# Two graph layers, attention in bursts: both quads of a batch weighed and scored together, with sums over key blocks kept in place

## The chip, the cores and the metric

The kernel runs on one core of a Trainium2 chip. The core has a matrix engine (TensorE, PE in the profile, with its weight loads as PEld), three engines for elementwise work (VectorE or DVE, ScalarE or ACT, GpSimd or POOL), and queues that start transfers between the chip's main memory (HBM) and its working memory (SBUF). Matmuls write to a third memory, PSUM, which has eight banks of 512 float32 columns; VectorE and ScalarE read it. The metric is the device time of one execution in microseconds, lower is better.

## The reference

Two layers over 64 batches of 256 nodes with 512 features, each with a residual: a graph attention layer with one head, and a masked attention with eight heads of 64. All is float32.

```python
h = relu(layernorm(x));   x = x + gat(h)        # layer 0
h = relu(layernorm(x));   x = x + mha(h)        # layer 1

def gat(X):                                      # W: 512 x 256, a: 2 x 256
    h = X @ W
    e = leaky_relu(h @ a[0] + (h @ a[1]).T, 0.2)
    alpha = softmax(e masked where adj == 0)
    return concat([alpha @ h, h], -1)

def mha(h):                                      # 8 heads of 64
    q, k, v = heads(h @ Wq.T + bq), heads(h @ Wk.T + bk), heads(h @ Wv.T + bv)
    attn = softmax(where(adj == 0, -inf, q @ k.T / 8))
    return merge(attn @ v) @ Wo.T + bo
```

One adjacency matrix of 256 x 256 serves all batches.

## The kernel before

**Tiling and names.** The 64 batches are taken in `NG` = 32 groups of `GB` = 2. The 256 nodes of a batch are `NT` = 2 blocks of 128 partitions, the features `HP` = 4 blocks of 128. Eight heads make two "quads" of `QH` = 4 heads. `bounded` is the program that runs; `any_inputs` is a second program for inputs out of bounds, which doesn't run here.

**Products.** The projections to q, k and v (`project`, tiles `pq`, `pk`, `pv`) and the output projection (`outputs`, tile `py`) use seven products of half-sized blocks in place of eight. `operand_sums` makes four sums of blocks of the left operand (tile `sums` for q, k, v, on GpSimd; tile `o_sums` for the output, on VectorE), `weight_sums` makes those of the weights once, and `seven` says which block meets which. A product adds into a PSUM bank that is kept over several products (`held_bank`) or into one of the five banks of the tag `turn`, which `mm` hands out. Totals, weighed values, scores and the layer-0 products come from `turn` too. A float32 matmul shows in the trace as two passes.

**Attention of layer 1.** `scores(g, b, quad)` makes, for four heads of a batch, the transposed scores (keys on partitions): tile `sc`, matmuls of 64 rows (two heads side by side in the array), 512 columns for both key blocks. ScalarE takes the exponential into `p`, VectorE multiplies two heads at a time by the mask `maskT`, GpSimd adds the two key blocks into the tile `ps`. `weigh(g, b, quad, p, ps)` is called a step later: a matmul with ones (128 x 32) sums `ps` over the keys into `total`, VectorE takes the reciprocal `r`, sixteen matmuls with 128 x 32 blocks of v make the weighed values `pr`, and VectorE multiplies them by `r` into `oT`. After the second quad, `operand_sums` makes `o_sums` from the two `oT` tiles, and the output products of that batch can start.

**Layer 0.** `first_norm(g)` normalises and transposes x (by way of VectorE's block transposes and HBM, tiles `xn`, `xt`, `passed`, `moved`, `hT`). `first_layer(g)` makes `ph` = h @ W, then from a transposition `pn` the weights `e` (ScalarE, VectorE for leaky relu, ScalarE for the exponential, VectorE for the mask), then `po`, the weighed sum, and the second layernorm with its transposition.

**Order.** TensorE's order is the order in which the program calls `matmul` and `transpose`: each is tied to the one before. On the other engines a call by way of `not_sooner` stays behind the call before it; other calls are placed by the planner, by when it expects their inputs. The pieces are interleaved by strings, one for each step; a group has four steps (batch and quad):

```python
steps = ("Snuuuuonuouuo", "Sssnunosunosnouso", "Sususuososuos", "Ssusuonusonuouunous")
```

At the beginning of a step the quad of the step before is weighed. Then `S` is `scores` of this step, `u` a piece of the next group's projections (one product of seven), `o` a piece of the output products of the last batch weighed, `s` a piece of `first_layer` of the group after next, `n` a piece of a later group's first norm. So weighing and scores stand together four times in a group: totals, values and scores of one quad each.

**Buffers.** `p`, `ps`, `r`, `oT0` and `oT1` have one buffer each. `turn` has five PSUM banks.

Of the kernel before, what the change touches and what calls it, by code (L numbers as in the profile page):

```python
# [14 lines left out]
P = 128  # L15
# [42 lines left out]
def bounded(  # L58
# [102 lines left out]
    bad = const.tile([P, 2, NT], F32, name="bad")  # L161
    a_b = att.tile([P, 2, F1], F32, tag="ps", name="a_b", bufs=1)
    nc.sync.dma_start(
# [84 lines left out]
    gpsimd.memset(rexp, -0.5)  # L248
    ones = const.tile([P, P], F32, name="ones")
    gpsimd.memset(ones, 1.0)  # L250

    def weight_sums(name):
# [6 lines left out]
    def last_bias():  # L259


        wide = att.tile([P, 2, 2, P], F32, tag="kept", name="bv_wide")
        for q in range(NQ):
            for half in range(2):
                gpsimd.tensor_scalar(
                    wide[:, half, q, :], ones, bv_col[:, half, q : q + 1], None, op0=ALU.mult
                )
        yield
        pb = mm("pb")
        for q in range(NQ):  # L270
            for half in range(2):
                matmul(
                    pb, wide[:, half, q, :], w_sb["o"][:, half, 2 * q : 2 * q + 2, :],
                    start=(q == 0 and half == 0), stop=(q == NQ - 1 and half == 1),
                )
        yield
        not_sooner(vector, "tensor_add", b_out, pb, b_out)
        yield


    def judge():
# [41 lines left out]

        room = att.tile([P, D], F32, tag="ps", name="squares", bufs=1)

# [26 lines left out]
        total = mm("total")[:, :10]  # L352
        matmul(total, ones, part, start=True, stop=True)
        norm = const.tile([P, 10], F32, name="norm")
# [40 lines left out]
    def stats(mv, src, t, name):  # L395
        st = small.tile([P, 6], F32, tag="st", name=f"st{name}_{t}")
        if vector.last:
            not_sooner(vector, "bn_stats", st, src[t])
        else:
            vector.bn_stats(st, src[t])  # L400
        vector.bn_aggr(mv[:, t, :], st)

    def norm_T(src, mv, name, by_pe):
# [7 lines left out]
        def factors(b):  # L411
            tiles = slice(b * NT, (b + 1) * NT)
            ve = small.tile([P, NT], F32, tag="ve", name=f"ve{name}_{b}")
            vector.tensor_scalar(ve, mv[:, tiles, 1], EPS, None, op0=ALU.add)
            less = small.tile([P, NT], F32, tag="less", name=f"less{name}_{b}")
            vector.tensor_scalar(less, mv[:, tiles, 0], -1.0, None, op0=ALU.mult)
            rstd = small.tile([P, NT], F32, tag="rstd", name=f"rstd{name}_{b}")
            gpsimd.tensor_tensor(rstd, ve, rexp, op=ALU.pow)
            gpsimd.tensor_tensor(less, less, rstd, op=ALU.mult)
            factor[b] = less, rstd  # L420
# [51 lines left out]
    def operand_sums(engine, quads, sums):  # L472
        a11, a12, a21, a22 = quads
        not_sooner(engine, "tensor_add", sums[:, 0], a21, a22)
        engine.tensor_sub(sums[:, 1], sums[:, 0], a11)
        not_sooner(engine, "tensor_sub", sums[:, 2], a11, a21)
        engine.tensor_sub(sums[:, 3], a12, sums[:, 1])

    def seven(quads, sums):

        a11, a12, _, a22 = quads
        s1, s2, s3, s4 = (sums[:, i] for i in range(4))
        return {
            1: (a11, W11), 2: (a12, W21), 3: (s4, W22), 4: (a22, T4),
            5: (s1, T1), 6: (s2, T2), 7: (s3, T3),
        }
# [5 lines left out]
    def first_norm(g):  # L495

        xt = {}
        mv = small.tile([P, GT, 2], F32, tag="mv", name=f"mv0_{g}")
        factors, norm, turn, fetch, put = norm_T(xt, mv, f"0_{g}", g == 0)
# [34 lines left out]
    def first_layer(g):  # L534
# [30 lines left out]
        yield  # L565
        mv = small.tile([P, GT, 2], F32, tag="mv", name=f"mv1_{g}")
        factors, norm, turn, fetch, put = norm_T(xt, mv, f"1_{g}", g == 0)
        for r in range(GT):
            b, t = divmod(r, NT)
            po = mm(f"po_{g}_{r}")[:, : F1 + 1]  # L570
            for kb in range(NT):
# [3 lines left out]
                )  # L575
            ri = small.tile([P, 1], F32, tag="ri", name=f"ri_{g}_{r}")
            not_sooner(vector, "reciprocal", ri, po[:, F1:])
# [14 lines left out]
        hT = big.tile([P, HP, TOK], F32, tag="hT1", name=f"hT1_{g}")  # L592
        sums = big.tile([P, 4, 2, N], F32, tag="sums", name=f"sums_{g}", bufs=1)
        quads = [
# [111 lines left out]

    def scores(g, b, quad):


        (q, q_tag), (k, k_tag) = (qkv[name, g, b] for name in "qk")  # L710
        name = f"{g}_{b}_{quad}"
        p = att.tile([P, QH, NT, N], F32, tag="p", name=f"p_{name}", bufs=1)
        ps = att.tile([P, QH, N], F32, tag="ps", name=f"ps_{name}", bufs=1)
        for i in range(QH // 2):
            hp = quad * QH // 2 + i
            sc = [mm(f"sc_{name}_{2 * i + j}").rearrange("p (k n) -> p k n", k=NT) for j in range(2)]
            for kb in range(NT):
                for j in range(2):
                    rows = slice(j * DH, (j + 1) * DH)
                    matmul(  # L720
                        sc[j][:, kb, :], k[rows, hp, kb * P : (kb + 1) * P], q[rows, hp, :],
                        start=True, stop=True,
                    )
            pair = p[:, 2 * i : 2 * i + 2]
            for j in range(2):
                not_sooner(scalar, "activation", pair[:, j], sc[j], AF.Exp, scale=scale)
            vector.tensor_mul(pair, pair, maskT[:, None, :, :].to_broadcast([P, 2, NT, N]))
            not_sooner(
                gpsimd, "tensor_add", ps[:, 2 * i : 2 * i + 2, :], pair[:, :, 0, :], pair[:, :, 1, :]
            )  # L730
        if quad == NQ - 1:
            places.extend((q_tag, k_tag))
        return p, ps

    oTs = {}

    def weigh(g, b, quad, p, ps):


        v, v_tag = qkv["v", g, b]  # L740
        name = f"{g}_{b}_{quad}"
        total = mm(f"total_{name}")[:, :N]
        for j in range(QH):
            matmul(
                total[j * S : (j + 1) * S, :], ones[:, :S], ps[:, j, :], start=True, stop=True
            )
        r = att.tile([P, N], F32, tag="r", name=f"r_{name}", bufs=1)
        vector.reciprocal(r, total)
        pr = mm(f"pr_{name}").rearrange("p (h n) -> p h n", h=2)
        for half in range(2):  # L750
            for kb in range(NT):
                for j in range(QH):
                    c0 = (quad * QH + j) * DH + half * S
                    matmul(
                        pr[j * S : (j + 1) * S, half, :], v[:, kb, c0 : c0 + S], p[:, j, kb, :],
                        start=(kb == 0), stop=(kb == NT - 1),
                    )
        oT = big.tile([P, 2, N], F32, tag=f"oT{quad}", name=f"oT_{name}", bufs=1)
        vector.tensor_mul(oT, pr, r[:, None, :].to_broadcast([P, 2, N]))
        oTs[quad] = oT  # L760
        if quad == NQ - 1:
            places.append(v_tag)
            quads = [oTs[c][:, :, r * P : (r + 1) * P] for r in range(2) for c in range(2)]
            sums = big.tile([P, 4, 2, P], F32, tag="o_sums", name=f"o_sums_{g}_{b}", bufs=1)
            operand_sums(vector, quads, sums)
            operands["o", g, b] = seven(quads, sums)

# [96 lines left out]

    steps = ("Snuuuuonuouuo", "Sssnunosunosnouso", "Sususuososuos", "Ssusuonusonuouunous")
    waiting, late = None, iter(())
    for g in range(NG):
        products = project(g + 1) if g + 1 < NG else iter(())
        pieces = first_layer(g + 2) if g + 2 < NG else iter(())
        for step, parts in enumerate(steps):  # L870
            b, quad = divmod(step, NQ)
            if g == step == 0:

                parts = "Snn" + parts[2:].replace("uon", "unon", 1)
            if waiting is not None:
                weigh(*waiting)
                if waiting[2] == NQ - 1:
                    late = outputs(*waiting[:2])
            for part in parts:
                if part == "u":  # L880
# [3 lines left out]
                elif part == "s":  # L884
                    next(pieces, None)
                elif part == "n":
                    next(norms, None)
                else:
                    waiting = (g, b, quad, *scores(g, b, quad))
            if step == 0 and g + 1 < NG:  # L890
                residual(g + 1)
            if step % 2 == 0 and g + 3 < NG:
                load(g + 3, b)
        run(products)
# [374 lines left out]
```

## Time and profile before

| | |
|---|---|
| time, median of three runs | 2532.96 us (2532.34 to 2534.09) |
| span of the profiled execution | 2530.6 us |
| TensorE busy | 2500.6 us, 99% |
| VectorE busy | 1772.5 us, 70% |
| ScalarE busy | 1008.3 us, 40% |
| GpSimd busy | 952.0 us, 38% |
| DMA, mean over the span | 81 GB/s |
| instructions | 41538, of these 16158 matmul passes |

The profile is that of one execution. A row of its groups says: line, engine, operation, output<-inputs by tile name, shapes, count, then busy us and mean ns of one, then the idle time of the engine just before these instructions and what ended most of it. A line of the timeline has the start in us, the us that a run of equal instructions took, engine, line, operation, tiles, shapes and count. Line 35 is the helper through which VectorE, ScalarE and GpSimd are called, line 137 the one for matmuls, so groups are told apart by their tiles. The end of a matmul is modelled, and ends overlap the starts that follow: on TensorE, compare starts.

### The profile page before, as it was taken

Reading aid. Unit: us, or ns where it says so; the run is one execution under the profiler, and the core shown is the slowest. Engines: PE = TensorE matmul, PEld = TensorE weight load, DVE = VectorE, ACT = ScalarE, POOL = GpSimd, SP = SyncE. Lnnn points to the kernel's source line nnn. Section 1 sums busy time; section 2 is a strip of 40 time slices with the busy share of each in tenths; the row PEclk is TensorE's granted clock in tenths of the full one; section 3 lists DMA queues with packets and bytes.
Section 4 is the critical chain, followed back from the end, with each engine's and each line's share of the span. In section 5 each row is a group of like instructions: output and inputs, shape, how many; then the busy total and the mean of one; then the engine's idle time right before and its main releaser. Section 6 shows DMA issues by size and latency. Waiting matters only on the chain.

```text
span 2530.6 us, 41538 instructions
## 1 busy us (share of the span) xinstructions
PE 2500.6 (99%) x16158; PEld 2024.7 (80%) x16158; DVE 1772.5 (70%) x2971; ACT 1008.3 (40%) x2019; POOL 952.0 (38%) x913
## 2 busy tenths in 40 slices
PE   8899999999999999999999999999999999999998
PEld 7687888888788888888887888888888878888875
DVE  6577766776767777667767677776677676777655
ACT  5444334343343343343433433433434334334321
POOL 3433334333344333343333443333433334433332
PEclk9999999999999999999999999999999999999999
DMA  6222122331232321223312323212233123232100
GB/s 187 67 84 83 60 84 84 92 100 59 67 101 76 101 84 60 83 84 92 101 59 67 101 76 100 86 60 82 84 92 100 59 68 100 76 101 86 37 29 35
DMA packets 129352, 205.39 MB, mean 81 GB/s; under 512 B 13952, under 2 KB 78208, under 8 KB 129152
## 3 DMA queue, kind: packets, MB, share of 16 engines
q1 hardware_dynamic: 129152, 202.69, 25.5%
q8 instruction: 129, 2.11, 0.3%
q14 instruction: 71, 0.58, 0.1%
HBM read 104.08 MB, written 98.57 MB: 80 GB/s over the span
## 4 chain that ended last, share of the span: by engine, by line
PE 97%; DVE 1%; DMA 1%; POOL 0%; issue 0%; ACT 0%; SPq 0%; DVEq 0%; ACTq 0%; POOLq 0%
PE pq L137 15%; PE pk L137 15%; PE pv L137 15%; PE py L137 15%; PE sc L137 10%; PE ph L137 9%; PE pr L137 9%; PE po L137 4%; PE total L137 3%; PE pn L140 1%; DMA w_sb<-in_L_gnn_W_dram 0%; DVE p L35 0%; POOL ps L35 0%; PE gram_q L137 0%; PE gram_k L137 0%
## 5 line engine op out<-in xcount | busy, mean ns | idle before, releaser
L35 POOL TENSOR_TENSOR ps<-p 128x512 f32<-128x512 f32 x256 | 416.6, 1642 | 698.9 <-DVE p L35 698.9
L35 DVE TENSOR_TENSOR x<-py,x 128x256 f32<-128x256 f32 x448 | 186.5, 416 | 313.8 <-PE py L137 307.2
L35 ACT ACTIVATE p<-sc 128x512 f32<-128x512 f32 x512 | 264.3, 603 | 273.7 <-PE sc L137 273.7
L35 DVE TENSOR_TENSOR p<-p,maskT 128x1024 f32<-128x1024 f32 x256 | 333.7, 1334 | 49.5 <-ACT p L35 49.5
L35 ACT ACTIVATE xn<-x,less,rstd 128x512 f32<-128x512 f32 x256 | 194.9, 813 | 316.5 <-POOL less L35 316.5
L137 PE MATMUL sc<-q,k 64*128 64x256 f32 x2048 | 266.8, 390 | 0.0
L137 PE MATMUL py<-wo_sb,o_sums 128*128 128x256 f32 x1024 | 262.7, 380 | 2.6 <-DVE x L35 2.6
L35 DVE RECIPROCAL r<-total 128x256 f32<-128x256 f32 x128 | 224.6, 1755 | 44.6 <-PE total L137 44.6
L137 PEld LDWEIGHTS sc<-q,k 64*128 64x128 f32 x2048 | 195.9, 186 | 72.1 <-issue 52.6
L35 POOL TENSOR_TENSOR rstd<-ve,rexp 128x2 f32<-128x2 f32 x128 | 91.6, 716 | 428.9 <-DVE less L35 428.9
L137 PE MATMUL pr<-p,v 128*32 128x256 f32 x4096 | 245.5, 379 | 0.0
L137 PE MATMUL pv<-wv_sb,sums 128*128 128x256 f32 x1024 | 241.7, 379 | 2.7 <-ACT kept_v L35 2.7
L137 PE MATMUL ph<-w_sb,hT 128*128 128x258 f32 x1024 | 242.7, 384 | 0.4 <-ACT hT L35 0.3
L137 PE MATMUL pq<-sums,wq_sb 128*128 128x256 f32 x1024 | 238.2, 381 | 4.1 <-POOL sums L35 4.1
L137 PE MATMUL pk<-sums,wk_sb 128*128 128x256 f32 x1024 | 239.9, 382 | 0.0
L137 PEld LDWEIGHTS ph<-w_sb,hT 128*128 128x128 f32 x1024 | 191.8, 190 | 38.3 <-ACT p L35 9.6
L137 PEld LDWEIGHTS pk<-sums,wk_sb 128*128 128x128 f32 x1024 | 191.8, 190 | 35.8 <-issue 10.7
L137 PEld LDWEIGHTS pq<-sums,wq_sb 128*128 128x128 f32 x1024 | 195.3, 191 | 31.2 <-POOL sums L35 4.5
L137 PEld LDWEIGHTS pv<-wv_sb,sums 128*128 128x128 f32 x1024 | 194.5, 190 | 29.5 <-ACT kept_v L35 3.1
L137 PEld LDWEIGHTS py<-wo_sb,o_sums 128*128 128x128 f32 x1024 | 191.9, 190 | 29.1 <-DVE x L35 3.4
L137 PEld LDWEIGHTS pr<-p,v 128*32 128x32 f32 x4096 | 134.6, 110 | 86.7
L137 PE MATMUL py<-wo_sb,oT 128*128 128x256 f32 x768 | 197.1, 380 | 2.8 <-DVE x L35 2.8
(120 smaller groups left out, 3710.0 us busy)
## 6 DMA issues: line engine op xcount, KB each, us to landing
passed<-xt SPq DMA_DIRECT2D x124, 512.0 KB, 2.7
moved<-passed SPq DMA_DIRECT2D x496, 128.0 KB, 3.6
x<-in_x_dram SPq DMA_DIRECT2D x64, 512.0 KB, 4.9
out_dram<-x SPq DMA_DIRECT2D x64, 512.0 KB, 3.8
wq_sb<-in_L_gnn_Wq_dram SPq DMA_DIRECT2D x2, 512.0 KB, 9.4
wk_sb<-in_L_gnn_Wk_dram SPq DMA_DIRECT2D x2, 512.0 KB, 10.9
wv_sb<-in_L_gnn_Wv_dram SPq DMA_DIRECT2D x2, 512.0 KB, 7.5
wo_sb<-in_L_gnn_Wo_dram SPq DMA_DIRECT2D x8, 128.0 KB, 3.8
```

The lines of the kernel that those rows point to most:

```text
L35: instruction = getattr(self.engine, operation)(*args, **kwargs)
L137: in_order(nc.tensor.matmul(*args, **kwargs))
L140: in_order(nc.tensor.transpose(*args))
```

## The change

Two things are changed, and some tiles are moved or cut so that they fit.

First, `scores` and `weigh` take a whole batch. A group has two steps in place of four, with the same pieces in the same order but two `S` fewer. At the beginning of a step, TensorE does total, pr, total, pr (both quads of the batch before), and then eight heads of scores. The purpose is that the kinds of matmul that use the array in tiles (128 x 32 and 64 x 128) stand together half as often.

Second, with exponentials p0 and p1 of the two key blocks and values v0 and v1, p0 v0 + p1 v1 = (p0 + p1) v0 + p1 (v1 - v0). GpSimd's sum p0 + p1 is written over p0, so that the tile `ps` goes and `p` can hold eight heads. In return `value_differences` subtracts the first block of v from the second, in place, on GpSimd, once for each batch, in the middle of a group's first step. `total` reads its sums from `p`.

Third, for space: a21 - ... of the operand sums is written over a block that is not read again, so `sums` and `o_sums` have three blocks in place of four; the ones for `total` are 32 columns, and a square of ones lives for a while in the place of `o_sums`; setup tiles (`a_b`, `squares`) live in the places of `oT0` and `oT1`; small tiles are put together or have fewer buffers.

```diff
-    a_b = att.tile([P, 2, F1], F32, tag="ps", name="a_b", bufs=1)
+    a_b = big.tile([P, 2, F1], F32, tag="oT0", name="a_b", bufs=1)
...
-    ones = const.tile([P, P], F32, name="ones")
+    ones = const.tile([P, S], F32, name="ones")
     gpsimd.memset(ones, 1.0)
+    square_ones = big.tile([P, P], F32, tag="o_sums", name="square_ones", bufs=1)
+    gpsimd.memset(square_ones, 1.0)
...
-        st = small.tile([P, 6], F32, tag="st", name=f"st{name}_{t}")
+        st = small.tile([P, 6], F32, tag="st", name=f"st{name}_{t}", bufs=4)
...
-        not_sooner(engine, "tensor_sub", sums[:, 2], a11, a21)
-        engine.tensor_sub(sums[:, 3], a12, sums[:, 1])
+        not_sooner(engine, "tensor_sub", a21, a11, a21)
+        engine.tensor_sub(sums[:, 2], a12, sums[:, 1])
...
+    def value_differences(g):
+        for b in range(GB):
+            v = qkv["v", g, b][0]
+            not_sooner(gpsimd, "tensor_sub", v[:, 1, :], v[:, 1, :], v[:, 0, :])
+
-    def scores(g, b, quad):
+    def scores(g, b):
...
-        p = att.tile([P, QH, NT, N], F32, tag="p", name=f"p_{name}", bufs=1)
-        ps = att.tile([P, QH, N], F32, tag="ps", name=f"ps_{name}", bufs=1)
-        for i in range(QH // 2):
+        p = att.tile([P, NQ * QH, NT, N], F32, tag="p", name=f"p_{name}", bufs=1)
+        for i in range(HP):
...
-                gpsimd, "tensor_add", ps[:, 2 * i : 2 * i + 2, :], pair[:, :, 0, :], pair[:, :, 1, :]
+                gpsimd, "tensor_add", pair[:, :, 0, :], pair[:, :, 0, :], pair[:, :, 1, :]
...
-    def weigh(g, b, quad, p, ps):
+    def weigh(g, b, p):
...
+        for quad in range(NQ):
...
-                total[j * S : (j + 1) * S, :], ones[:, :S], ps[:, j, :], start=True, stop=True
+                    total[j * S : (j + 1) * S, :], ones, p[:, quad * QH + j, 0, :],
+                    start=True, stop=True,
...
-    steps = ("Snuuuuonuouuo", "Sssnunosunosnouso", "Sususuososuos", "Ssusuonusonuouunous")
+    steps = ("Snuuuuonuouuossnunosunosnouso", "Sususuososuossusuonusonuouunous")
...
-        for step, parts in enumerate(steps):
-            b, quad = divmod(step, NQ)
+        for b, parts in enumerate(steps):
...
             if waiting is not None:
                 weigh(*waiting)
-                if waiting[2] == NQ - 1:
-                    late = outputs(*waiting[:2])
+                late = outputs(*waiting[:2])
...
-            if step == 0 and g + 1 < NG:
-                residual(g + 1)
-            if step % 2 == 0 and g + 3 < NG:
-                load(g + 3, b)
+                if i == len(parts) // 2:
+                    if b == 0:
+                        if g + 1 < NG:
+                            residual(g + 1)
+                        value_differences(g)
+                    if g + 3 < NG:
+                        load(g + 3, b)
```

## The prediction

> **What bounds the kernel now.** I read the page first: busy shares, then the chain that ended last, then the costliest groups.
>
> ```profile
> PE 2500.6 (99%) x16158; PEld 2024.7 (80%) x16158; DVE 1772.5 (70%) x2971; ACT 1008.3 (40%) x2019; POOL 952.0 (38%) x913
> ...
> PE 97%; DVE 1%; DMA 1%; POOL 0%; issue 0%; ACT 0%; SPq 0%; DVEq 0%; ACTq 0%; POOLq 0%
> ...
> L35 DVE TENSOR_TENSOR p<-p,maskT 128x1024 f32<-128x1024 f32 x256 | 333.7, 1334 | 49.5 <-ACT p L35 49.5
> ...
> L35 DVE RECIPROCAL r<-total 128x256 f32<-128x256 f32 x128 | 224.6, 1755 | 44.6 <-PE total L137 44.6
> ...
> L35 POOL TENSOR_TENSOR x<-x,b_out 128x512 f32<-128x512 f32 x128 | 158.7, 1268 | 0.0
> ```
>
> The chain is TensorE from end to end. So only two things move the time: passes, or extra time between passes, on TensorE; and whatever makes TensorE wait. The change keeps the number of matmuls. So I looked at how passes follow each other, in the timeline of TensorE alone around one round of attention (total, pr, sc):
>
> ```profile
> 1035.44 1.89 PE L137 MATMUL pq<-hT,wq_sb 128*128 128x256 f32 x8
> 1037.17 1.89 PE L137 MATMUL pq<-sums,wq_sb 128*128 128x256 f32 x8
> 1038.89 1.03 PE L137 MATMUL py<-wo_sb,o_sums 128*128 128x256 f32 x4
> 1039.85 0.64 PE L137 MATMUL total<-ps,ones 128*32 128x256 f32 x8
> 1040.31 1.91 PE L137 MATMUL pr<-p,v 128*32 128x256 f32 x32
> 1042.14 2.00 PE L137 MATMUL sc<-q,k 64*128 64x256 f32 x16
> 1044.07 3.75 PE L137 MATMUL ph<-w_sb,hT 128*128 128x258 f32 x16
> 1047.66 0.59 PE L137 MATMUL pk<-hT,wk_sb 128*128 128x256 f32 x2
> ```
>
> Starts tell, not durations (their ends overlap). Eight full passes take 1.72 to 1.73 us, 0.2155 each. Four of py should take 0.86; the next start comes after 0.96, so going from 128*128 to 128*32 costs 0.10. Two rows of four concurrent passes of total take 0.46 (0.43 + 0.03). Eight such rows of pr take 1.83 (1.72 + 0.10), eight pairs of sc 1.93 (1.72 + 0.20), and the sixteen ph passes (258 columns) 3.59 against 3.48 (+0.11). The costs gather where the tile shape changes: 0.10 + 0.10 + 0.20 + 0.11, about 0.5 us a round. There are two rounds to a batch, 64 batches.
>
> Three rounds of a group of two batches last 4.22 us from total to the next 128*128 product. The one that opens the second batch lasts 4.60. Its timeline:
>
> ```profile
> 1059.85 1.57 ACT L35 ACTIVATE e<-pn,H 128x256 f32<-128x256 f32 x4
> 1060.32 0.64 PE L137 MATMUL total<-ps,ones 128*32 128x256 f32 x8
> ...
> 1060.77 1.37 DVE L35 SCALAR_TENSOR_TENSOR e<-e 128x512 f32<-128x512 f32 x2
> 1060.77 1.91 PE L137 MATMUL pr<-p,v 128*32 128x256 f32 x32
> 1061.48 1.32 ACT L35 ACTIVATE e<-e 128x512 f32<-128x512 f32 x2
> 1062.06 1.75 DVE L35 RECIPROCAL r<-total 128x256 f32<-128x256 f32 x1
> ...
> 1062.61 2.38 PE L137 MATMUL sc<-q,k 64*128 64x256 f32 x16
> 1063.73 1.22 DVE L35 TENSOR_TENSOR e<-e,maskT 128x512 f32<-128x512 f32 x2
> 1063.78 2.06 ACT L35 ACTIVATE p<-sc 128x512 f32<-128x512 f32 x4 [0.97 <-PE sc L137]
> ...
> 1064.87 0.68 DVE L35 TENSOR_TENSOR oT<-pr,r 128x512 f32<-128x512 f32 x1
> ```
>
> The next product starts at 1064.92, so sc takes 2.31 instead of 1.93. The `turn` tag has five PSUM banks; total, pr and three scores fill them, the fourth score needs the bank of total, and that is free when the reciprocal has read it, at 1062.06 + 1.75 = 1063.81. The matmul starts 0.05 later. The reciprocal is late because the layer-0 work on e, made just before, sits ahead of it on VectorE. This 0.38 us repeats in 29 of 32 groups: 11 us.
>
> **What the Trainium skill says.** TensorEngine Tiling (Array Packing), Key Properties: changing the tiling mode drains TensorE; the trace agrees, with 0.10 to 0.20 at each change. Perfetto Trace Analysis, Optimization Strategy: the same gap again and again on the saturated engine can mean that there is no SBUF or PSUM for the next tile; that is the 0.38. VectorE: DVE Perf Modes, First, the fixed hardware budget: reciprocal is an iterated divide; the trace has 1755 ns for 256 columns where a product of 512 (oT) takes 684. SBUF — State Buffer, Who interferes with whom: a VectorE instruction with two SBUF inputs contends with a GpSimd one that reads SBUF; an o_sums add takes 1.41 us at 1024.05, beside GpSimd's sums, and 0.41 at 1066.60.
>
> **The change part by part.**
> *One burst a batch.* 64 rounds' worth of shape changes go: each 0.51, less about 0.02 for total after pr. 64 x 0.49 = 31.4 us off.
> *The old wait* goes with its round: 29 x 0.38 = 11.1 us off; what replaces it comes below.
> *The burst and its banks.* With T the start of the first total, and the pieces above: total 1 to 0.46, pr 1 to 2.20, total 2 to 2.66, pr 2 to 4.49, then four pairs of scores at 4.49, 5.46, 6.32, 7.19, end 8.15. Twelve banks are asked for, and five exist. Five are taken by the first score. The seven others must wait for readers. `r` has one buffer, so VectorE goes reciprocal 1, oT 1, reciprocal 2, oT 2.
> Bursts that open a first batch: reciprocal 1 at 0.71 (1040.56 in the timeline, total at 1039.85) to 2.46; oT 1 after pr 1, to 3.3; reciprocal 2 to 5.05, oT 2 to 5.75. ScalarE's exponentials start 1.17 after the scores (1063.78 against 1062.61): 5.66 to 6.26, then one every 0.49. Fourth score, needed at 5.46: reciprocal 2, free. Fifth and sixth at 6.32: oT 2 and exponential 1, just free. Eighth at 7.19: exponential 3 at 7.29. I put 0.15 on each of 31 bursts: 4.7 us on.
> Bursts that open a second batch have e ahead: reciprocal 1 from 1.74 (1062.06) to 3.50, e's mask products 3.41 to 4.63, oT 1 to 5.23, reciprocal 2 from 5.15 to 6.91. The fourth score at 5.46 has no bank. The next to come free is that of the first score, after exponential 1 at 6.26 (6.31 with the hand-over), then exponential 2 at 6.75, then reciprocal 2. So the wait is 0.85, and since two interleaved scores fall out of step it costs about 0.11 more (0.28 late at 1063.86 made 0.38 before): 1.0 us, in 29 groups: 29 us on. Behind the waiting matmul stands everything of TensorE; nothing overtakes it. Which bank is given is the planner's choice; I take the one freed first, since the fourth score's wait of before is also on the first freed.
> *Sums in place, differences of values.* GpSimd's add keeps its size (1642 ns) and only writes elsewhere. 64 subtractions of 128x512 are new, unseen in this form: between 1268 (x, b_out) and 1642 (ps), say 1.3, 83 us in all on an engine 38% busy. Queued behind them are the next layer-0 adds; only the next burst's pr waits for them, some 20 us on. Cost nothing. The same holds for the mask products and adds that now come four in a row: their reader is half a group away.
> *Smaller tiles* (st, mv, factor, ri, in-place a21, `ones` cut to 32 columns): the same instructions or one memset more; nothing.
> *Both ends.* At the start TensorE stands 4.15 us at 105.80 for GpSimd's sums; four more scores (1.73) are moved ahead of that: 1.7 off. In the last group TensorE waits four times 1.2 to 1.6 for x adds queued behind mask products (0.7 more in all for ps); one such wait a batch, longer, takes their place, and the last burst is 2 us longer before the last products: I take 1.6 off.
> Sum: 2533.0 - 31.4 - 11.1 + 4.7 + 29.0 - 3.3 = 2520.9, say 2521 us.
>
> **The rivals.**
> A, above: 2521, 0.45.
> B, the wait that grows: the fourth score gets the bank of total 2. Then 6.96 instead of 6.31: 1.6 a group, 29 x 0.6 = 17.4 more: 2538.4, slower than before by 0.21%. For it: in the old round the fourth score waited for a reciprocal. Against: there it was the first bank free. 0.25.
> C, VectorE becomes the bound of that burst: as B, and a mask product (1.2 us) goes ahead of oT 2, as one goes ahead of the o_sums at 1065.47; the fifth score waits another 0.9: 29 x 0.9 more, about 2564. 0.16.
> D, no bank wait to speak of (VectorE's order puts e's products behind, or scores get other banks): A less 29 x 0.85: 2496. Against: the same work on e stands in the same place. 0.14.
>
> **How the numbers follow.** The time is A's. Faster by over 0.2% (below 2527.9): A but for a fifth, and D: 0.50. Within: a fifth of A, and of B, which lies on the edge, nearly half: 0.20. Slower: the rest of B, and C: 0.30. The range runs from D to the near part of C, with 0.1 a round (6 us) on the shape changes within it: 2499 to 2548.
>
> **What would show it.** Right: 64 stretches of total, pr, total, pr, sc in a row; 8.1 to 8.3 us from total to the next 128*128 product in the bursts of first batches, some 9.2 in those of second batches, where the gap lies inside sc and ends at an exponential; 77.3 us a group falling to about 77.0. B shows 9.8, the gap ending at a reciprocal. C shows over 10. Wrong would be: no saving between pr of the first quad and total of the second (a start-to-start of 0.31 there instead of 0.22), or new waits outside the bursts, on kept, po or sums.

## The result, and the profile after

The changed kernel takes 2576.61 us (median of four runs, 2572.74 to 2577.51), the one before 2533.34 beside it: ratio 1.0168 (1.0151 to 1.0186). It is 1.7% slower; 2521 us had been predicted, and 2548 was the upper end of the range.

The page of the changed kernel: rows that answer to those shown of before, and two new ones (of `pq` and of `hT`):

```profile
PE 2508.6 (97%) x16158; PEld 2052.2 (80%) x16158; DVE 1856.3 (72%) x2971; ACT 1014.4 (39%) x2019; POOL 1069.4 (42%) x978
...
PE 87%; DVE 7%; ACT 3%; issue 1%; DMA 1%; SPq 1%; POOL 0%; ACTq 0%; DVEq 0%
...
L35 DVE TENSOR_TENSOR p<-p,maskT 128x1024 f32<-128x1024 f32 x256 | 419.7, 1679 | 0.0
...
L137 PE MATMUL pq<-hT,wq_sb 128*128 128x256 f32 x1024 | 243.9, 386 | 22.2 <-ACT kept_q L35 22.2
...
L35 DVE RECIPROCAL r<-total 128x256 f32<-128x256 f32 x128 | 224.7, 1755 | 50.2 <-PE total L137 43.4
...
L35 ACT COPY hT<-moved 128x512 f32<-128x512 f32 x248 | 141.1, 618 | 188.0 <-DMA moved<-passed 188.0
```

The chain of waits has left TensorE for 13% of the span; before, it left it for 3%. Three rows say where to look. A mask product takes 1679 ns where it took 1334. TensorE waits 22.2 us in all for `kept_q` on ScalarE, a wait that before doesn't have. And ScalarE waits 188 us for the transfers `moved<-passed` before its copies to `hT`; in before it was 4.8 us. (`kept_q` is one of the tiles `kept`, of which there are two buffers: ScalarE copies a finished product of q there, which frees its PSUM bank, and VectorE adds it to another product later, which frees the buffer.)

First the bursts, which were most of the prediction. The timeline of a burst that opens a second batch (some lines of TensorE, VectorE and ScalarE):

```profile
1076.32 0.64 PE L137 MATMUL total<-p,ones 128*32 128x256 f32 x8
...
1076.77 1.91 PE L137 MATMUL pr<-p,v 128*32 128x256 f32 x32
...
1078.06 1.75 DVE L35 RECIPROCAL r<-total 128x256 f32<-128x256 f32 x1
...
1078.50 0.61 PE L137 MATMUL total<-p,ones 128*32 128x256 f32 x8
...
1078.93 1.91 PE L137 MATMUL pr<-p,v 128*32 128x256 f32 x32
...
1080.77 1.56 PE L137 MATMUL sc<-q,k 64*128 64x256 f32 x10
...
1081.94 1.08 ACT L35 ACTIVATE p<-sc 128x512 f32<-128x512 f32 x2 [3.13 <-PE sc L137]
...
1082.59 2.88 PE L137 MATMUL sc<-q,k 64*128 64x256 f32 x22 [0.26 <-ACT p L35]
...
1085.39 1.99 PE L137 MATMUL pk<-hT,wk_sb 128*128 128x256 f32 x8
```

From the first total to the next square product: 1085.39 - 1076.32 = 9.07 us. The scores start 4.45 after the total, stop after ten passes, and go on when an exponential has freed its bank. From the first pr to the second total there is no price for a change of shape (1.73 us for eight rows of passes, 0.216 each). All this is as case A had it, and it is not where the time went.

The timeline of a burst that opens a first batch, with what goes before and after it on all engines and on the transfer queue (SPq):

```profile
1028.20 0.38 SPq L35 DMA_DIRECT2D passed<-xt  x1
...
1033.86 0.42 DVE L35 TENSOR_TENSOR x<-py,x 128x256 f32<-128x256 f32 x1 [0.17 <-PE py L137]
...
1034.36 0.40 SPq L815 DMA_DIRECT2D out_dram<-x  x1
...
1034.86 2.27 SPq L457 DMA_DIRECT2D moved<-passed  x4
...
1035.48 0.64 PE L137 MATMUL total<-p,ones 128*32 128x256 f32 x8
...
1039.93 4.33 PE L137 MATMUL sc<-q,k 64*128 64x256 f32 x32
1040.47 1.14 ACT L35 COPY hT<-moved 128x512 f32<-128x512 f32 x2 [4.30 <-DMA moved<-passed]
...
1041.52 4.00 ACT L35 ACTIVATE p<-sc 128x512 f32<-128x512 f32 x8
...
1041.69 1.27 POOL L35 TENSOR_TENSOR sums<-hT 128x512 f32<-128x512 f32 x1 [12.89 <-ACT hT L35]
1041.78 1.46 DVE L35 TENSOR_TENSOR o_sums<-oT,oT 128x256 f32<-128x256 f32 x1
...
1044.19 3.72 PE L137 MATMUL pq<-hT,wq_sb 128*128 128x256 f32 x16
...
1047.40 6.77 DVE L35 TENSOR_TENSOR p<-p,maskT 128x1024 f32<-128x1024 f32 x4
...
1053.79 1.03 PE L137 MATMUL py<-wo_sb,oT 128*128 128x256 f32 x4
1054.10 0.68 DVE L35 TENSOR_TENSOR q<-pq,kept_q 128x512 f32<-128x512 f32 x1
...
1054.87 0.84 ACT L35 ACTIVATE kept_q<-pq,bq_sb 128x256 f32<-128x256 f32 x2 [4.35 <-PE py L137]
...
1055.76 1.99 PE L137 MATMUL pq<-hT,wq_sb 128*128 128x256 f32 x8 [0.94 <-ACT kept_q L35]
```

Read it from the top. The second half of the layer-1 transposition is sent out at 1028.20 (`passed`). Its return (`moved`) stands on the queue behind the write of the finished batch (`out_dram`), and that write waits for the last x add, at 1033.86. So the return is issued at 1034.86 and lands for ScalarE at 1040.47, 5.0 us after the total. On ScalarE the copy stands ahead of the exponentials: these could start 1.17 after the first score (1039.93), at 1041.10, but start at 1041.52, and the scores wait for their banks. GpSimd's sums of `hT` start at 1041.69 and slow VectorE's o_sums, four operations of 1.4 to 1.5 us each in place of 0.4. The mask products start at 1047.40, beside GpSimd's adds, and last 6.77 us. The q add behind them frees a buffer of `kept` only at 1054.78, so the next copy to `kept_q` is late: TensorE's next product starts at 1055.76, 1.1 us after the four passes of 1053.79 (0.86) are through.

In the kernel before, the same stretch of the transfer queue reads:

```profile
1087.82 0.38 SPq L35 DMA_DIRECT2D passed<-xt  x1
1091.59 1.73 SPq L456 DMA_DIRECT2D moved<-passed  x4
...
1097.94 0.40 SPq L806 DMA_DIRECT2D out_dram<-x  x1
```

There the return stands ahead of the write, 3.77 us after the sending. The order of the two on the queue is the planner's, and the change turned it round, in 29 of the 32 groups.

An account by stages, from TensorE's starts in the profiled executions (us; "30 groups" runs from the first burst of the second group to that of the last; "write behind" and "and pn sooner" are the first and the fifth experiment below):

| | before | after | write behind | and pn sooner |
|---|---|---|---|---|
| start, to the first burst of the second group | 170.50 | 173.73 | 172.74 | 169.94 |
| 30 groups | 2307.60 | 2341.13 | 2299.19 | 2284.14 |
| of these: bursts of first batches, mean | - | 8.73 | 8.31 | 8.31 |
| bursts of second batches, mean | - | 9.07 | 9.07 | 8.57 |
| everything outside the bursts, sum | - | 1807.2 | 1777.9 | 1777.9 |
| last group | 52.5 | 59.5 | 59.1 | 58.1 |

After less before: 3.2 at the start, 33.5 in the groups, 7.0 in the last group, 43.8 us in all. "Bursts" are counted from the first total to the next square product.

### The profile page after: what moved, and what is told of

It reads as the page before. It is cut to its first block, busy times and chain, and to the rows that moved or that the text cites. A ratio compares the mean times of both kernels' runs of the same rounds, so it can differ in the third digit from the quotient of the medians.

```text
span 2574.4 us, 41412 instructions
## 1 busy us (share of the span) xinstructions
PE 2508.6 (97%) x16158; PEld 2052.2 (80%) x16158; DVE 1856.3 (72%) x2971; ACT 1014.4 (39%) x2019; POOL 1069.4 (42%) x978
## 4 chain that ended last, share of the span: by engine, by line
PE 87%; DVE 7%; ACT 3%; issue 1%; DMA 1%; SPq 1%; POOL 0%; ACTq 0%; DVEq 0%
PE pk L137 15%; PE py L137 14%; PE pv L137 14%; PE pq L137 13%; PE ph L137 9%; PE sc L137 8%; PE pr L137 7%; PE po L137 4%; DVE p L35 3%; PE total L137 2%; ACT p L35 1%; DMA moved<-passed 1%; DVE r L35 1%; DVE o_sums L35 1%; ACT kept_q L35 1%
## 5 line engine op out<-in xcount | busy, mean ns | idle before, releaser
L35 POOL TENSOR_TENSOR p<-p 128x512 f32<-128x512 f32 x256 | 447.3, 1767 | 528.6 <-DVE p L35 528.6
L35 DVE TENSOR_TENSOR p<-p,maskT 128x1024 f32<-128x1024 f32 x256 | 419.7, 1679 | 0.0
L35 ACT ACTIVATE xn<-x,factor 128x512 f32<-128x512 f32 x256 | 194.4, 807 | 354.6 <-POOL factor L35 354.6
L137 PE MATMUL pq<-hT,wq_sb 128*128 128x256 f32 x1024 | 243.9, 386 | 22.2 <-ACT kept_q L35 22.2
L137 PE MATMUL pk<-hT,wk_sb 128*128 128x256 f32 x1024 | 244.9, 382 | 0.0
L137 PEld LDWEIGHTS pq<-hT,wq_sb 128*128 128x128 f32 x1024 | 190.6, 191 | 67.1 <-ACT kept_q L35 33.0
L137 PE MATMUL pv<-wv_sb,hT 128*128 128x256 f32 x1024 | 237.5, 380 | 1.3 <-ACT kept_v L35 1.3
L137 PEld LDWEIGHTS pk<-hT,wk_sb 128*128 128x128 f32 x1024 | 191.7, 190 | 36.1 <-issue 10.7
L137 PEld LDWEIGHTS py<-wo_sb,oT 128*128 128x128 f32 x1024 | 195.4, 191 | 29.1 <-issue 1.1
L137 PEld LDWEIGHTS pv<-wv_sb,hT 128*128 128x128 f32 x1024 | 194.9, 190 | 28.6 <-ACT kept_v L35 1.7
L35 ACT COPY hT<-moved 128x512 f32<-128x512 f32 x248 | 141.1, 618 | 188.0 <-DMA moved<-passed 188.0
```

Source lines behind the costliest of these rows:

```text
L35: instruction = getattr(self.engine, operation)(*args, **kwargs)
L137: in_order(nc.tensor.matmul(*args, **kwargs))
```

## The experiments

The theories: **Q**, the write ahead of the fetch on the transfer queue starts the loss in the groups. **V**, it is VectorE's load alone: mask products, o_sums and reciprocals of two quads in a row would make the wait on `kept` whenever the fetch comes. **C**, GpSimd's adds and differences beside VectorE's mask products make these late. **E**, the wait in second-batch bursts comes from the layer-0 work on e. **T**, in the last group the order on VectorE makes the new waits.

**The write behind the fetches.** The write of the finished batch is tied behind the return of the transposition; in the trace the order on TensorE, VectorE, ScalarE and GpSimd is that of the changed kernel, instruction for instruction; only the queue's differs.

```diff
-                nc.sync.dma_start(
+                last_moved[name] = nc.sync.dma_start(
                     moved[j * S : (j + 1) * S].rearrange("a i c t n -> a i (c t n)"),
                     passed[b].rearrange("(i a) j e -> j a i e", a=S)[j],
-                )
+                ).ins.name
...
-        nc.sync.dma_start(og[g, b], xt)
+        written = nc.sync.dma_start(og[g, b], xt)
+        if f"1_{g + 2 - b}" in last_moved and b == 0:
+            after(written, last_moved[f"1_{g + 2 - b}"])
```

> The changed kernel with one edit: on the queue of transfers, the write of a finished batch is put behind the fetches of the layer-1 transposition of the group after next, which it was planned ahead of. Theory Q (queue order is the root of the trouble at the first-batch bursts): ScalarE's hT copy comes some 3 us earlier, so the first-batch bursts last 8.2 to 8.4 us (8.3 to 9.8 now), GpSimd's operand sums leave the stretch of the mask products, and the wait for kept_q at about 19 us after the burst's start falls from 1.3 to under 0.6: 0.7 to 1.2 us a group, 2540 to 2555 us. Theory V (VectorE's own queue is the root: four mask products and the o_sums stand ahead of the q add, whatever the queue of transfers does): only the bursts get shorter, 0.3 us a group, and the wait for kept_q stays above 1: about 2566 us.

Measured: 2532.44 us (2530.1 to 2534.77), ratio to before 0.9994 (0.9985 to 1.0003). So 44 us come back, more than Q had said. Its timeline at the same place of a group:

```profile
1012.61 0.38 SPq L35 DMA_DIRECT2D passed<-xt  x1
...
1016.40 1.73 SPq L459 DMA_DIRECT2D moved<-passed  x4
...
1019.89 0.64 PE L137 MATMUL total<-p,ones 128*32 128x256 f32 x8
...
1020.87 1.14 ACT L35 COPY hT<-moved 128x512 f32<-128x512 f32 x2 [0.29 <-DMA moved<-passed]
...
1023.39 0.40 SPq L817 DMA_DIRECT2D out_dram<-x  x1
...
1027.49 0.43 DVE L35 TENSOR_TENSOR o_sums<-o_sums,oT 128x256 f32<-128x256 f32 x1
...
1028.51 6.77 DVE L35 TENSOR_TENSOR p<-p,maskT 128x1024 f32<-128x1024 f32 x4
...
1035.97 0.84 ACT L35 ACTIVATE kept_q<-pq,bq_sb 128x256 f32<-128x256 f32 x2 [1.45 <-DVE q L35]
```

The copy to `hT` comes 0.98 after the total (5.0 in the changed kernel). GpSimd's sums of `hT` are early too, three of the four o_sums take 0.4 us again, and the mask products start 8.6 after the total instead of 11.9. They are as long as before the repair, 6.77 us, so V's load is all there; but `kept_q` comes in time, and in the 30 groups TensorE waits nowhere outside the bursts. In the table the sum outside the bursts falls by 29.4 us, all of it at 27 waits of TensorE for `kept_q`, and the first-batch bursts go from 8.73 to 8.31, 12.6 us over 30 of them. Q holds for the groups; V, without the late fetch, costs nothing.

**One more buffer for q's third `kept`.** It takes the tag of `e`, which is free then.

```diff
-                s = att.tile([P, 2, N], F32, tag="kept", name=f"kept{i}_{name}_{g}")
+                tag = "e" if i == 2 and name == "q" else "kept"
+                s = att.tile([P, 2, N], F32, tag=tag, name=f"kept{i}_{name}_{g}")
```

> The changed kernel with one edit: the third kept tile of q goes to a buffer of the tag e (free at that time) instead of one of the two of the tag kept. Theory K (TensorE waits for kept_q because ScalarE has no buffer until VectorE has read the first kept tile): the wait of 1.3 us falls to nothing, 27 to 30 groups times 1.1, 2543 to 2548 us. Rival: the q adds on VectorE are late all the same and TensorE waits for one of them a product later; then the wait only moves, and the time stays above 2565 us.

Measured: 2544.76 (2543.5 to 2550.45), ratio 1.0052 (1.0036 to 1.0069). Outside the bursts the sum is 1777.9 us, to a tenth that of the first experiment, while first-batch bursts keep a mean of 8.78. So the loss in the groups has two parts that add: the wait on the buffer, 29.4 us, and banks that come late in the burst, 13 to 14.

**GpSimd's adds and differences left out.** The kernel leaves out the sums over key blocks and the differences of values; `total` then covers the first key block alone.

```diff
-            not_sooner(
-                gpsimd, "tensor_add", pair[:, :, 0, :], pair[:, :, 0, :], pair[:, :, 1, :]
-            )
...
-                        value_differences(g)
```

> The changed kernel without GpSimd's adds of the two key blocks and without the differences of values: the totals are those of the first key block alone and the values are weighed without the subtraction, so part of layer 1 is left out. It takes GpSimd away from beside the mask products. Theory C (contention between VectorE and GpSimd makes VectorE late): the mask products fall from 1679 ns to about 1200 to 1350, VectorE reaches the q add some 2 us earlier, the wait for kept_q goes: about 1.1 us a group, and the waits of the last group get shorter: 2530 to 2545 us. Rival V (the length of VectorE's queue, not its speed): the products stay near 1600 because the operand sums still run beside them, and the wait stays above 0.6: over 2555 us.

Measured: 2541.31 (2537.49 to 2542.71), ratio 1.003 (1.0018 to 1.0043). Its page:

```profile
L35 DVE TENSOR_TENSOR p<-p,maskT 128x1024 f32<-128x1024 f32 x256 | 324.7, 1309 | 0.6 <-ACT p L35 0.6
```

With mask products of 1309 ns the wait on `kept` is gone too (outside the bursts 1777.9), with the fetch as late as in the changed kernel (ScalarE's wait for it 179.7 us) and first-batch bursts of 8.78. The last group shrinks to 52.9 us. So C is a second condition: the wait on `kept` needs both the late fetch and the slowed mask products; either cure removes it whole, and so does the third buffer.

**The second part of the change by itself**, in the kernel before with its four bursts a group: sums in place, differences of values.

```diff
-                gpsimd, "tensor_add", ps[:, 2 * i : 2 * i + 2, :], pair[:, :, 0, :], pair[:, :, 1, :]
+                gpsimd, "tensor_add", pair[:, :, 0, :], pair[:, :, 0, :], pair[:, :, 1, :]
...
-                    total[j * S : (j + 1) * S, :], ones[:, :S], ps[:, j, :], start=True, stop=True
+                    total[j * S : (j + 1) * S, :], ones[:, :S], p[:, j, 0, :], start=True, stop=True
...
+                if step == 0 and i == len(parts) // 2:
+                    value_differences(g)
```

> The kernel before with the second part of the change alone: sums over key blocks written in place, differences of values on GpSimd (in the middle of the group's first step), totals from p. Four bursts a group as before. My theory: this part costs nothing while bursts are short, 2530 to 2537 us. Rival: the in-place sums and the 64 subtractions alone slow VectorE enough to make TensorE wait: over 2545 us.

Measured: 2534.49 (2533.01 to 2535.52), ratio 1.0003 (0.9994 to 1.0012), mask products 1334 ns as before. The rearranged sum costs nothing by itself, and the transfers keep the order of before. The third part, the smaller tiles, was not tried alone; in the groups nothing is left for it to cost, since with the write behind the fetches TensorE has no wait outside the bursts.

**pn sooner**, on top of the first experiment: in the string of a group's first step the last `s` goes ahead of the last `u`, so that the work on e is done eight passes earlier.

```diff
-    steps = ("Snuuuuonuouuossnunosunosnouso", "Sususuososuossusuonusonuouunous")
+    steps = ("Snuuuuonuouuossnunosunosnosuo", "Sususuososuossusuonusonuouunous")
```

> e1_fetch_first, and in the string of a group's first step the piece with pn stands one projection product sooner (the end reads nosuo in place of nouso), so VectorE's work on e is over before the burst of the second batch. Theory E (the 0.95 us wait inside that burst is due to e ahead of the reciprocals): its length falls from 9.08 to 8.2 to 8.5 us, 29 times 0.6 to 0.9: 2507 to 2516 us. Rival (five banks are too few whatever VectorE does): the burst stays above 8.9 and the time above 2527.

Measured: 2515.3 (2513.95 to 2517.86), ratio 0.993 (0.9914 to 0.9947). Second-batch bursts go from 9.07 to 8.57, 15 us over 30. One of them:

```profile
1050.63 0.64 PE L137 MATMUL total<-p,ones 128*32 128x256 f32 x8
...
1051.34 0.68 DVE L35 TENSOR_TENSOR e<-e,maskT 128x512 f32<-128x512 f32 x1
...
1051.94 1.75 DVE L35 RECIPROCAL r<-total 128x256 f32<-128x256 f32 x1
...
1059.19 1.99 PE L137 MATMUL pk<-hT,wk_sb 128*128 128x256 f32 x8
```

The first reciprocal starts 1.31 after the total (1.74 before the move). E holds for the most part: of the 0.76 by which these bursts were longer than first-batch ones, 0.50 is gone. The other 0.26 is left; the last of e's mask products still stands ahead of the reciprocal, but that it makes the 0.26 was not tried.

**The same move in the kernel before** ("Sssnunosunosnouso" to "Sssnunosunosnosuo").

> The kernel before, with only the pn piece one projection product sooner, as in e5_pn_sooner. If the 0.38 us wait in its third round comes from e ahead of the reciprocal, that round falls from 4.60 to 4.22 us: 11 us, 2520 to 2525 us. If not, 2532 or more.

Measured: 2522.65 (2522.29 to 2523.17), ratio 0.9957 (0.994 to 0.9973): 11.2 us, what the prediction had put on the old wait of 0.38. The third round of a group falls from 4.60 to 4.22 us. So of the 18.5 us by which the version above beats before (2515.3 against 2533.84), this line alone would give 11.2, and the change proper, with its queue put right, is worth the rest: 7 us, or 5 if the second measurement of that version (2518.35 against 2534.22, below) is taken. In the 30 groups of the profiled executions it is worth 12.4 us (2284.1 against 2296.5); the last group gives 5.5 of these back (58.1 against 52.6).

**Mask products later in the last group**, on top of the first experiment: each is called after a piece of the output products, not tied to it.

```diff
+            unmasked.append(pair)
+            if g < NG - 1:
+                mask_pair()
...
                     next(late, None)
+                    if unmasked:
+                        mask_pair()
```

> e1_fetch_first, and in the last group alone each mask product with its GpSimd add is issued after an output piece, one pair a piece, so that the x adds come between them. Theory T (the last group loses 7 us because the third output product waits 4.6 us for an x add behind four mask products, and the passes after so long a wait take 427 ns): the two waits of 4.6 us fall under 2, most of the 427 ns passes go, the last 60 us get 5 to 9 us shorter: 2523 to 2528 us. Rival: VectorE has the same work in the last group in any order, the wait only moves to the totals that need the masked exponentials: 2530 or more.

Measured: 2532.32, ratio 0.9994 (0.9985 to 1.0003), and TensorE's two waits are still 4.59 us. The planner had put the four mask products ahead of the x adds as before: the edit changed no order on VectorE, so it says nothing on T.

**All four edits together.**

> e1_fetch_first with the edits of e5_pn_sooner, e6_last_masks and e2_kept_e. If they are independent: 2532.4 less 21 less 6, and the buffer of e2_kept_e gives under 3 more once the fetch is in time: 2500 to 2508 us.

Measured: 2517.93 (2516.64 to 2518.41), ratio 0.9936 (0.9919 to 0.9952). The expectation fails by some 10 us: with the fetch in time the extra buffer adds nothing, and the last group's edit was void.

**The last group's order, tied.** On top of pn sooner, in the last group each mask product is tied behind the x add of one piece.

```diff
+    def behind_add(*args):
+        not_sooner(vector, "tensor_mul", *args)
...
                     next(late, None)
+                    if unmasked:
+                        mask_pair(behind_add)
```

> Theory T: in the last group the third output product waits 4.2 to 4.6 us, twice, because four mask products (6.8 us with what lies between) stand ahead of the x adds on VectorE, and the passes after the wait run at half speed. Here, in the last group alone, each mask product is tied behind one x add, so that the adds come first. T expects both waits to fall under 1.5 us, the passes of 427 ns after them to go, the last group to shorten by 6 to 9 us, and the time to be 2506 to 2511 us, against 2515.3 with the write behind the fetches and pn sooner alone. Rival, that the last total then waits for the mask products and GpSimd's adds by as much: 2513 to 2517.

> The same kernel as the one with the write behind the fetches and pn sooner, beside the one above on the same chip: 2513 to 2518 us.

Measured: 2516.22 (2514.18 to 2519.01) with the tie and 2518.35 (2514.62 to 2518.75) without, ratios 0.9933 (0.9919 to 0.9947) and 0.9936 (0.9922 to 0.9949); the last group is 58.2 and 58.3 us. No gain; the expectation of T fails. What the tie was to remove, in the timeline of the changed kernel:

```profile
2522.29 6.75 DVE L35 TENSOR_TENSOR p<-p,maskT 128x1024 f32<-128x1024 f32 x4
...
2523.23 1.99 PE L137 MATMUL py<-wo_sb,oT 128*128 128x256 f32 x8
...
2528.97 0.94 DVE L35 TENSOR_TENSOR x<-py,x 128x256 f32<-128x256 f32 x2
...
2529.44 2.07 PE L137 MATMUL py<-wo_sb,o_sums 128*128 128x256 f32 x4 [4.21 <-DVE x L35]
```

and what took its place, with the tie:

```profile
2488.11 0.42 DVE L35 TENSOR_TENSOR x<-py,x 128x256 f32<-128x256 f32 x1
...
2488.16 1.02 PE L137 MATMUL py<-wo_sb,oT 128*128 128x256 f32 x4
...
2488.27 1.26 POOL L35 TENSOR_TENSOR p<-p 128x512 f32<-128x512 f32 x1 [10.51 <-DVE p L35]
...
2488.44 2.17 DVE L35 TENSOR_TENSOR p<-p,maskT 128x1024 f32<-128x1024 f32 x1
...
2490.53 0.41 DVE L35 TENSOR_TENSOR x<-py,x 128x256 f32<-128x256 f32 x1
...
2491.00 1.13 PE L137 MATMUL py<-wo_sb,o_sums 128*128 128x256 f32 x4 [1.82 <-DVE x L35]
```

One wait of 4.21 has become three (1.82, 1.30, 1.30). Every mask product but the first now stands beside a GpSimd add and takes 2.17 us; the x add waits for that instead. The time is the rival's, though not for its reason: the x adds wait, not the last total. So this order gains nothing. The length of the mask products beside the adds is what is left: without those adds TensorE's two waits were 2.51 us in place of 4.59, from start to start, and the last group 52.9 us.

## Why the prediction was wrong, and where it was right

**Right: the bursts.** With the fetch in time (first experiment) first-batch bursts take 8.31 us (8.1 to 8.3 predicted), second-batch bursts 9.07 (9.2 predicted), the wait inside ends at an exponential, and a group takes 77.01 us (about 77.0 predicted). Over 30 groups that is 8.4 us less than before; the terms of the prediction, counted for 30 groups, make 7.0 (60 x 0.49 + 11.1 - 30 x 0.15 - 29). Case A was the right one of the four. The old wait of 0.38 was worth its 11 us (pn sooner in the kernel before), the in-place sums nothing (second part by itself).

**The step that failed: four mask products and adds in a row were put at nothing, because "their reader is half a group away".** That looked at the readers of the adds and products and not at what stands behind them in VectorE's order. Behind the mask products stands the q add, and it frees a buffer of `kept` for which TensorE waits a few pieces on. The prediction's timetable for the burst also took ScalarE's copy to `hT` where before has it, just after the total. It priced no change on the transfer queue, whose order the planner makes anew. The write went ahead of the fetch, and the copy came 4 us later. The first three experiments show it: 29.4 us of waits on `kept`, which need both the late fetch and the slowed mask products, and some 13 us in the bursts, which need the fetch alone. The mask products were taken at 1.2 us; in a row and beside GpSimd's adds they average 1.68. The prediction had named new waits on `kept` as a sign of being wrong, and 27 of them came.

**The ends, predicted at -3.3, came out at +10.2.** The last group was put at -1.6, with one wait "longer" than four of 1.2 to 1.6; it was +7.0. Four mask products (6.75 us) stand between scores and x adds, twice, and TensorE's waits in this group add up to 2.6 us more than before's; another 3.8 us are 18 passes at half speed after these waits, where before has none (last section). The prediction had no term for such passes. The start was put at -1.7 and came out at +3.2. That figure isn't only the kernel's: the pn-sooner program was profiled twice and had 169.94 and 172.07 us there. The earlier scores do shorten the wait for GpSimd's sums (4.53 to 3.70 us from start to start), but new waits of 1.5 and 1.66 us for `kept_v` follow, and 19 passes run at half speed where before has 5, which is 3.0 us. Some of that is chance: the kernel before with pn sooner, whose start is nearly the same as that of before, had 14. What of the start is due to the change was not tried.

**Still open:** why the planner turned the two transfers round. The traces show the order, not its reason; the second part of the change alone doesn't do it, and the longer bursts, the smaller tiles and the later calls of `residual` and `load` were not tried apart.

## What to carry to other kernels

When a stretch of the saturated engine's work is rearranged, list again what every other engine and every transfer queue has in order behind it: on the queue here a write that waited for its data held up the transfers behind it, and putting it behind them gave back 44 us. Work moved into a longer row has to be checked against the instruction queued behind the row, not only against its own reader. And where a plan is made by a planner, compare the queue orders before and after before believing that untouched parts stayed where they were.

## What the runs showed of the hardware

**Mask products have two lengths.** In the changed kernel 145 of the 256 take about 1.2 us and 111 about 2.3; before it was 227 and 29, with GpSimd's adds left out 233 and 22. A mean of 1.68 is a mixture, not a slower product. The length goes with which of the two engines starts first. In the trace of before, 97 mask products are joined by a GpSimd add that starts 0.15 to 0.17 us after them: they keep their 1.2 us, and the add takes 2.18. The 29 long ones start 0.17 to 0.18 us after an add: the add takes 1.38 us, the product 2.29. The Trainium skill (SBUF — State Buffer, Who interferes with whom) has the contention of the two engines as an exclusive lock; two lengths on both sides, with almost nothing between, agree with that.

**After a wait, passes at half speed.** After the waits of 4.59 us (start to start) in the last group of the changed kernel, 11 and 7 passes start 427 ns apart, not 216. The Trainium skill (TensorE: Matmul & The Clock Gate, What's actually happening) tells of a free-running window of about 3.4 us after which an idle array runs at half rate. The runs agree on the half rate and on the part of chance: a wait of 3.449 us at the start had no such pass after it and one of 3.464 in the same program had seven. They don't agree on the length: of two waits of 2.51 us in the run without adds, shorter than that window, the first had six such passes after it and the second none.
